# A macaron block on one core: Down's unpacking placed earlier in the first job, rows turned a step later, and a rearranged end

## The chip, the cores and the metric

The kernel runs on one core of one Trainium2 chip. A core has a matrix engine (TensorE, PE in the profile), a vector engine (VectorE, DVE), an activation engine (ScalarE, ACT), a general engine (GpSimd, POOL), and SyncE (SP), which here only issues transfers. They run side by side, each through its own instructions in order, and wait for each other by semaphores. Matrix products are written to PSUM, eight banks of 128 x 512 float32; everything else lies in SBUF, and transfers by DMA go between SBUF and DRAM. The metric is the device time of the whole kernel in microseconds, the median of several runs. Less is better.

## The reference

The input is 2 x 1024 tokens of 1024 features. Three sublayers follow each other: half a feed-forward, a state-space convolution, half a feed-forward.

```python
x = L0_attn_u
x = x + 0.5 * ffn(layernorm(x))
x = x + s4(layernorm(x))
x = x + 0.5 * ffn(layernorm(x))

def ffn(x):
    Wg, Wu, Wd = (dequant(...) for gate, up, down)   # 4-bit weights, a scale and a zero per 128 rows
    h = silu(xf @ Wg) * (xf @ Wu)                    # 1024 -> 2752
    return h @ Wd                                    # 2752 -> 1024

# dequant: W[k, n] = s[k // 128, n] * (w4[k, n] - (z4[k // 128, n] + 1))
# s4: a kernel K of length 1024 from its parameters, a causal convolution of each row with K, plus D * u
```

Eight 4-bit weights are packed in one 32-bit word along the rows of a weight matrix.

## The kernel before, in words

The 2048 tokens are four batches of 512. A feed-forward of one batch is a job, and there are eight: `JOBS = [(0, 1), (1, 1), (0, 3), (1, 3), (2, 1), (3, 1), (2, 3), (3, 3)]`, batch and sublayer. They are numbered 0 to 7 here. The convolution of a batch is woven into the first stage of a later job.

A job has two stages. Up (`gate_up`) takes 64 steps: eight waves of hidden columns, in each the eight groups of 128 input rows. Its input is the normalized batch, turned so that features lie on partitions, in two pieces of different precision (`xTh`, `xTl`), and each weight tile is multiplied with both. After each group the partial sums in PSUM (`pg`) are rescaled in place by a ratio of two groups' scales, some by ScalarE, some by VectorE (`scaled`, L811 and L815). So TensorE can only add the next group to a bank when that bank's rescale is done. At the end of a wave ScalarE and VectorE form `hf`, and GpSimd splits it in two pieces, `hh` and `hl`. Down (`down`) takes 44 steps, two halves of the output columns by 22 tiles of hidden rows. A step has four column groups `c` with two products each, into four banks `po`, with a rescale after each except for the last two of a half: tile 20 has none behind it, and after tile 21 (one product, the short tile) the result is scaled into `y`.

The weights of a step are signed bytes read from DRAM four steps ahead (`load_bytes`, L772 for Up, L779 for Down) and cast to float three steps ahead by GpSimd (`make_weights`, L788; in job 0 some by ScalarE, L786). The bytes are made once, during job 0: the packed words are fetched, their nibbles unpacked by VectorE with six operations (`signed_bytes`: two of L625, two of L629 that add the zero points, two of L632), copied by GpSimd (L670 for Up's eight blocks, L704 for Down's), and stored to DRAM (L676, L712). Down's words come in six blocks, three for each half of the output columns, named `rawd` in the profile, and in this text the first to the sixth. The third and the sixth have 88 rows instead of 128.

Instructions that belong to other work are hung on steps: `up` and `dn` are tables of hooks, run when the step's instructions are written; a number with a half is a hook in the middle of a step. `first_weights` hangs the unpacking. Its table `blocks` has a row per block: when its words are fetched, when the six VectorE operations come, when the eight copies; each second copy is followed half a step later by a store. The numbers count from Up step 52, and from 12 on they are Down steps less 12. What is written inside `in_order_of_writing`, `in_pieces` or `pinned` keeps its order on the named engine; everything else is ordered by a scheduler that works with estimated costs. So the order in which the engines finally run differs from the text, and where this text says that one instruction stands before another, it is the order of the built program. Fetches are moved forward by it as soon as their buffer is free. SyncE issues nearly all transfers of the kernel in one order, and a store that waits for its data holds up the loads behind it.

Job 0's Down stage also prepares job 1. The rows of batch 1 get their moments (L189, L192), `r` from `ve` by GpSimd (L205), a correction of `r` in four small VectorE operations, the first of them `e` (L218), the normalization by VectorE (`normalize`, L265), and they are turned by `turn_by_pool`: four transposes on TensorE (L239), a copy by ScalarE (L257), two operations of GpSimd (L258, L259). In jobs 1, 2, 5 and 6 the same correction for the batch of the job before is hung on the last steps of Up.

Results go back to the rows in two ways. In most stages `y` is turned by VectorE and DRAM. In the first half of job 0 and the second half of job 7 it is done by `back_by_products`: four transposes on TensorE (L1014) into a bank, and a sum on VectorE (L1016) onto the row tile `x`. The kernel ends with four of these, one for each tile of 128 rows, each followed by a store of its half row.

Of the kernel before, what the change touches and what calls it, by code (L numbers as in the profile page):

```python
# [57 lines left out]
def macaron_s4_kernel(  # L58
# [67 lines left out]
    def give_back(*tiles):  # L126
        for tile_ in tiles:
            i = held.pop(id(tile_))
            turn_of.remove(i)
            turn_of.append(i)  # L130
# [585 lines left out]
    def first_weights(up, dn, at):  # L716

        for w in range(1, len(WAVES)):  # L720
            s0 = (0, 4, 8 * w - (14 if w < 5 else 15))[min(w, 3) - 1]
            steps = (0.5, 1, 2.5, 3, 3) if w == 1 else range(6)
            in_pieces(at, [(up, s0 + d) for d in steps], lambda w=w: split(w))
            copies = {1: (3, 3, 3.5, 3.5) + (3.5,) * 4, 2: (3, 3, 4, 4, 5.5, 5.5, 6, 6)}
            copies = copies.get(w, (3, 3, 4, 5, 6, 6, 7, 8))
            if 1 < w < len(WAVES) - 1:
                both = lambda w=w: (fetch(w + 1), fetch_zeros(w + 1))
                at(up, s0 + (3 if w == 2 else 6), lambda both=both: in_order_of_writing(both, ET.SP))
            for k, d in zip(EVEN_FIRST, copies):
                at(up, s0 + d, lambda w=w, k=k: dequantize(w, k))  # L730
            for odd, o in enumerate({1: (3.5, 3.5), 2: (5.5, 7)}.get(w, (6.5, 9.5))):
                at(up, s0 + o, lambda w=w, odd=odd: keep_bytes(w, odd))
        s0 = len(STEPS) - 12

        def when(d):
            return (up, s0 + d) if d < 12 else (dn, d - 12)

        blocks = (
            (-3, (-1, -0.5, 0, 0.5, 1, 1.5), (1, 1, 2, 3, 4, 5, 6, 7)),
            (1, (3.5, 4, 5, 5.5, 6.5, 7.5), (8, 9, 10, 11, 12, 12, 13, 14)),  # L740
            (9, (13.5, 15, 16.5, 17.5, 19, 19.5), (18, 18, 18.5, 19, 20, 20, 21, 21.5)),
            (15, (20.5, 22, 23.5, 24, 25, 25.5), (24.5, 24.5, 25, 25.5, 26, 26.5, 27, 27.5)),
            (22, (27, 28.5, 30, 31, 31.5, 32.5), (31.5, 31.5, 32, 32.5, 33, 33.5, 34, 34.5)),
            (29, (35, 37, 39, 39.5, 41, 41.5), (40, 40.5, 41, 41.5, 42, 42.5, 43, 43.5)),
        )
        for k, (fetched, split_at, copied) in enumerate(blocks):
            a, rt = divmod(k, 3)
            at(*when(fetched), lambda a=a, rt=rt: fetch_down(a, rt))
            in_pieces(at, [when(d) for d in split_at], lambda a=a, rt=rt: split_down(a, rt))
            for i, (j, d) in enumerate(zip(EVEN_FIRST, copied)):  # L750
                at(*when(d), lambda a=a, rt=rt, j=j: dequantize_down(a, rt, j))
                if i % 2:
                    half = lambda a=a, rt=rt, i=i: keep_bytes_down(a, rt, i // 4, i // 2 % 2)
                    at(*when(d + 0.5), half)
# [180 lines left out]
    def down(j, b, hooks):  # L935

        steps = [(a, f) for a in range(NH) for f in range(NF)]
        for d, (a, f) in enumerate(steps):
            w = next_weights()
            for hook in hooks.get(d, ()):  # L940
                hook()
            if f == 0:
                ps = [acc(f"po_{j}_{a}_{c}") for c in range(4)]
            for c in range(4):
                if c == 2:
                    for hook in hooks.get(d + 0.5, ()):
                        hook()
                for k, part in enumerate(reversed(h[f])):
                    nc.tensor.matmul(  # L949
                        ps[c],  # L950
                        w[:, bass.ts(c, P)],
                        part,
                        start=(f == 0 and k == 0),
                        stop=(f == NF - 1),
                        skip_group_check=True,
                    )
                on_act = c % 2 == 0 or (j == 0 and c == 1 and f % 2 == 0)
                on_act = on_act or (c == 1 and d in relief.get(j, ()))
                if f < GD - 1:
                    scaled(on_act, ps[c], ps[c], ratd[:, 4 * a + c, f : f + 1])  # L960
                elif f == NF - 1:
                    if c == 0:
                        yT[a] = ypool.tile([P, 4 * TB], F32, tag="y", name=f"y_{j}_{a}")
                    if by_products(j, a):
                        y = yT[a][:, bass.ts(c, TB)]
                        scaled(on_act, y, ps[c], ratd[:, 4 * a + c, GD - 1 :])
                    else:
                        y, p = block_of(yT[a], c), ps[c].rearrange("p (t i) -> p t i", i=Q)
                        scaled(on_act, y, p, ratd[:, 4 * a + c, GD - 1 :])
                    give_back(ps[c])  # L970
        h.clear()

    by_products = lambda j, a: (j, a) in ((0, 0), (len(JOBS) - 1, NH - 1))
    y_dram = [dpool.tile([TB, 512], F32, tag=f"yz{a}", name=f"yz{a}") for a in range(NH)]
# [622 lines left out]
    def fast():  # L1597
        def store_half(t, a, queue):

            own = bass.ts(a, 512)  # L1600
            queue.dma_start(rows_of(out, JOBS[-1][0])[t][:, own], x[JOBS[-1][0]][t][:, own])

        for j, (b, k) in enumerate(JOBS):
# [4 lines left out]
            def at(hooks, s, f):  # L1608
                hooks.setdefault(s, []).append(f)

            if prev:
# [9 lines left out]
                if pk == 1:  # L1621
# [50 lines left out]
                    steps += [(up, start_ + gap * 3 + 14.5), (up, start_ + gap * 3 + 15)]  # L1672
                    in_pieces(at, steps, lambda: moments_by_tile(pb, 3, True, LIFT))
                    done = start_ + gap * 3 + 15
                    steps = [(up, done + 0.5 + i / (2 if j == 1 else 1)) for i in range(4)]
                    in_pieces(at, steps, lambda: deviations_in_pieces(pb, 3))

                    def save():
# [38 lines left out]
            if after:  # L1717
                ab, ak = after
                if ak == 1:
                    at(up, 55 if j == 0 else 6, lambda: load_x(ab, rows_of(u, ab)))  # L1720
                    if j == 0:
                        steps = [(dn, d) for d in (2.5, 4, 6, 9, 10.5, 14.5, 16, 17.5, 18.5)]
                        in_pieces(at, steps, lambda: moments_by_tile(ab, 1, True, LIFT))
                        steps = [(dn, 21 + i / 2) for i in range(4)]
                        in_pieces(at, steps, lambda: deviations_in_pieces(ab, 1))
                    else:
                        steps = [(up, s) for s in range(12, 21)] + [(up, 20.5)]
                        in_pieces(at, steps, lambda: moments_by_tile(ab, 1, True, LIFT))
                        steps = [(up, s) for s in range(21, 25)]
                        in_pieces(at, steps, lambda: deviations_in_pieces(ab, 1))  # L1730
                turns = {}

                def turning(t):
                    if t not in turns:
                        turns[t] = [], []
                        turns[t] += (turn_by_dma(ab, t, turns[t][1]),)
                    rest = turns[t][1] or turns[t][2:]
                    next(rest[0], None)

                for t in range(NT):  # L1740
                    for half in range(2):
                        d, where = (24 + 4 * t + 2 * half if j == 0 else (2, 6, 14, 20)[t] + half), dn
                        if j > 1:
                            d, where = (54 if ak == 3 else 25) + 2 * t + half, up
                        piece = lambda t=t, half=half: normalize(ab, t, half)
                        piece = lambda piece=piece: in_order_of_writing(piece, ET.DVE)
                        at(where, d, piece)
                    if j == 0:
                        for half in range(2):
                            piece = lambda t=t, half=half: turn_by_pool(ab, t, half)  # L1750
                            at(dn, 26 + 4 * t + 2 * half, piece)
                        continue
                    late = (12, 13) if t == NT - 1 else (13, 17)
                    for d in (1, 2, 3, 5, 6, 7, 9) + late:
                        piece = lambda t=t: turning(t)
                        piece = lambda piece=piece: in_order_of_writing(piece, ET.Pool, ET.SP)
                        at(dn, 2 + 9 * t + d + (j == 1 and t == 0), piece)
# [18 lines left out]
            down(j, b, dn)  # L1776
            assert all(s in (0, 0.5) or 0 <= s < len(STEPS) and s * 2 % 1 == 0 for s in up)
            assert all(0 <= d < NH * NF and d * 2 % 1 == 0 for d in dn)
        for t in range(NT):
            back_by_products(b, 1, t)  # L1780
            store_half(t, 1, (nc.sync, nc.scalar)[t % 2])

    STARTING = ET.Activation, ET.DVE, ET.SP
    first = {}
# [205 lines left out]
```

## Time and profile before

| What | Value |
|---|---|
| Runs, us | 2036.26, 2033.29, 2035.08; median 2035.08 |
| The profiled execution, us | 2036.95 |
| Its span, us | 2035.2 |
| Granted clock of TensorE, mean of the span | 0.998 |
| Job 0: Up's last products, Down's last products | about 185 us, 276.9 us |
| Busy of GpSimd, 240 to 250 us | 10.0 of 10 |
| Waits of PE for VectorE's rescales, whole span (Up, Down) | 4.7 us in 11, 3.1 us in 4 |
| Waits of GpSimd's casts for bytes of Down, whole span | 8.4 us in 5, 5.4 us in 3 of them in job 0 |
| TensorE's last product of Down | 2023.4 us |

The span runs from the first to the last instruction of the program; the time of an execution lies some 1.75 us above it. The time of runs differs by 3 us between the lowest and the highest. A line of the profile names the line of the kernel, the engine, the operation, and the tiles written and read (`po<-po,ratd`), with numbers of batch and step left out; a wait is put down to what ended it. PE's matmul times overlap, so that a product that is listed with 0.39 us follows the one before by 0.21 to 0.23 us.

### The profile page before, as it was taken

The page shows a single profiled execution, that of the slowest core. Times are in us where ns is not written, and L with a number is a line of the kernel's source. Part 1 is how long each engine was busy: PE and PEld are TensorE (multiplying, and loading weights), DVE is VectorE, ACT ScalarE, POOL GpSimd, SP SyncE. Part 2 cuts the span into 40 slices and gives each one's busy share as a digit, 9 for nine tenths or more (in the row PEclk, how much of TensorE's full clock was granted, in tenths as well). Part 3 has the DMA queues.
Part 4 walks back from the last instruction along what each step waited for, and adds up shares of the span by engine and source line. Part 5 has one row for each costly group of instructions (what it writes and reads, how often), then busy time and mean ns, then how long its engine had stood idle before and what let it go on. Part 6 is the DMA issues. An engine that isn't in the chain of part 4 may idle for free.

```text
span 2035.2 us, 29665 instructions
## 1 busy us (share of the span) xinstructions
PE 2004.1 (98%) x9202; PEld 1374.5 (68%) x9202; DVE 1631.0 (80%) x2710; ACT 1416.2 (70%) x2221; POOL 1371.5 (67%) x1771
## 2 busy tenths in 40 slices
PE   7999999999999999999999999999999999999998
PEld 4656766577766677656866578667686676866576
DVE  8987878868888778877778777887878878777776
ACT  7888787747775577777767776764776647767775
POOL 6977868748765577655976578754686646965542
PEclk9999999999999999999999999999999999999999
DMA  5343332343524236311552126242263331661113
GB/s 166 119 136 99 110 103 62 79 103 92 148 63 102 73 71 196 120 30 35 143 161 85 33 50 172 79 93 83 50 161 93 84 90 38 160 187 34 35 37 102
DMA packets 345965, 197.13 MB, mean 97 GB/s; under 512 B 166989, under 2 KB 323670, under 8 KB 345798
## 3 DMA queue, kind: packets, MB, share of 16 engines
q1 hardware_dynamic: 344206, 192.55, 34.9%
q10 hardware_dynamic: 1464, 2.20, 0.3%
q8 instruction: 75, 1.23, 0.3%
q14 instruction: 92, 0.75, 0.1%
q0 software_dynamic: 128, 0.39, 0.1%
HBM read 127.52 MB, written 48.57 MB: 87 GB/s over the span
## 4 chain that ended last, share of the span: by engine, by line
PE 93%; DVE 3%; POOL 1%; issue 1%; ACT 1%; DMA 0%; ACTq 0%; POOLq 0%; DVEq 0%
PE pg L855 58%; PE po L949 30%; PE pc L1317 3%; PE pb L1317 1%; ACT pg L811 1%; DVE pg L815 1%; DVE po L815 0%; POOL w_up L788 0%; DVE rawd L629 0%; POOL r L205 0%; DVE hf L890 0%; POOL hl L897 0%; DVE rawd L632 0%; DVE stats L1797 0%; POOL q L670 0%
## 5 line engine op out<-in xcount | busy, mean ns | idle before, releaser
L811 ACT ACTIVATE pg<-pg,rat 128x512 f32<-128x512 f32 x1280 | 807.1, 661 | 383.6 <-PE pg L855 378.8
L815 DVE TENSOR_TENSOR pg<-pg,rat 128x512 f32<-128x512 f32 x1128 | 748.2, 692 | 146.5 <-PE pg L855 139.1
L855 PE MATMUL pg<-xTh,w_up 128*128 128x512 f32 x2752 | 844.4, 435 | 3.9 <-DVE pg L815 2.7
L855 PE MATMUL pg<-xTl,w_up 128*128 128x512 f16 x2752 | 708.0, 381 | 2.5 <-DVE pg L815 2.0
L855 PEld LDWEIGHTS pg<-xTh,w_up 128*128 128x128 f32 x2752 | 518.4, 189 | 167.5 <-DVE pg L815 7.7
L788 POOL CAST w_up<-b 128x768 fp32r<-128x768 int8 (+2 forms) x491 | 376.6, 773 | 356.9 <-PE pg L855 259.1
L811 ACT ACTIVATE po<-po,ratd 128x512 f32<-128x512 f32 x669 | 438.2, 662 | 145.3 <-PE po L949 144.6
L949 PE MATMUL po<-hl,w_down 128*128 128x512 f32 x1344 | 527.5, 393 | 3.5 <-DVE po L815 3.1
L949 PE MATMUL po<-hh,w_down 128*128 128x512 f32 x1344 | 523.4, 390 | 0.0
L815 DVE TENSOR_TENSOR po<-po,ratd 128x512 f32<-128x512 f32 x611 | 424.4, 696 | 112.1 <-PE po L949 111.2
L855 PEld LDWEIGHTS <-w_up 128*128 128x128 bf16 x2752 | 226.7, 98 | 340.2 <-issue 156.1
L788 POOL CAST w_down<-bd 128x512 fp32r<-128x512 int8 x352 | 217.8, 623 | 151.6 <-PE po L949 73.7
L949 PEld LDWEIGHTS po<-hl,w_down 128*128 128x128 f32 x1344 | 252.5, 188 | 64.0 <-DVE po L815 8.3
L949 PEld LDWEIGHTS po<-hh,w_down 128*128 128x128 f32 x1344 | 252.8, 188 | 51.3
L897 POOL TENSOR_TENSOR hl<-hf,hh 128x512 fp32r<-128x512 f32 x168 | 217.1, 1292 | 7.1
L896 POOL CAST hh<-hf 128x512 fp32r<-128x512 f32 x168 | 108.3, 645 | 81.1 <-DVE hf L890 62.3
L890 DVE SCALAR_TENSOR_TENSOR hf<-pg,rat,g 128x512 f32<-128x512 f32 x168 | 121.1, 746 | 40.5 <-ACT g L887 34.3
L887 ACT ACTIVATE g<-pg,rat 128x512 f32<-128x512 f32 x168 | 110.1, 688 | 33.7 <-PE pg L855 17.8
L1002 POOL TENSOR_TENSOR x<-x,yr 128x512 f32<-128x512 f32 x52 | 66.8, 1284 | 0.0
L291 POOL TENSOR_TENSOR lo<-x,hi 128x512 f16<-128x512 f32 x48 | 62.0, 1291 | 0.0
L189 DVE BATCH_NORM_STATS2 stats<-x 128x6 f32<-128x512 f32 x88 | 60.0, 681 | 0.0
L289 POOL TENSOR_TENSOR mid<-hi,top 128x512 bf16<-128x512 f32 x48 | 56.0, 1167 | 0.0
(214 smaller groups left out, 1081.2 us busy)
## 6 DMA issues: line engine op xcount, KB each, us to landing
b<-wq SPq DMA_DIRECT2D x319, 96.0 KB
bd<-wdq SPq DMA_DIRECT2D x336, 64.0 KB
x<-in_L_attn_u_dram SPq DMA_DIRECT2D x30, 512.0 KB
yz<-y SPq DMA_DIRECT2D x56, 256.0 KB
yr<-yz SPq DMA_DIRECT2D x56, 256.0 KB
b<-wq SPq DMA_DIRECT2D x128, 64.0 KB
sz<-xn SPq DMA_DIRECT2D x16, 512.0 KB
st<-sz SPq DMA_DIRECT2D x64, 128.0 KB
```

Of the source, the lines that this page charges most:

```text
L291: nc.gpsimd.tensor_tensor(lo[:, own], n[:, own], hi[:, own].bitcast(F32), ALU.subtract)
L788: nc.gpsimd.tensor_copy(t, b)
L811: nc.scalar.activation(dst, src, AF.Copy, scale=sc)
L815: nc.vector.tensor_tensor(dst, src, sc.to_broadcast(list(dst.shape)), ALU.mult)
L855: product = lambda: nc.tensor.matmul(p, weights, (lo, hi)[k][:, g, :], start=(g == 0 and not done), stop=(g == GK - 1 and done), skip_grou ...
L887: nc.scalar.activation(g, pg, AF.Silu, scale=rat[:, 2 * f, GK - 1 :])
L890: nc.vector.scalar_tensor_tensor(hf, pu, last, g, ALU.mult, ALU.mult)
L896: nc.gpsimd.tensor_copy(hi, hf)
L897: nc.gpsimd.tensor_tensor(lo, hf, hi.bitcast(F32), ALU.subtract)
L949: nc.tensor.matmul(ps[c], w[:, bass.ts(c, P)], part, start=(f == 0 and k == 0), stop=(f == NF - 1), skip_group_check=True,)
L1002: nc.gpsimd.tensor_tensor(part, part, rows_back.pop((a, t)), ALU.add)
L1317: nc.tensor.matmul(dst, lhsT, rhs, start=start, stop=stop, skip_group_check=True)
```

## The change

Five places are edited.

- The table `blocks`: every number is lower, so the words of Down are fetched, unpacked, copied and stored sooner: two steps for the first block, three to three and a half for the third to fifth, four to five and a half for the sixth.
- In job 0 the normalization and the turning of batch 1's rows come one step later each.
- In jobs 2, 5 and 6 the first `e` operation comes one step later, at Up step 51.5, and the last of the four stays at 53.5. In job 1 the new formula gives the old steps.
- In the last job's second half, the last two tiles of hidden rows are handled together by a new function, `last_steps`: for each column group its three products, one behind the other, then the scaling into `y`. VectorE takes groups 0 and 2, ScalarE group 1, and group 3 is halved between them.
- At the very end the transposes of row tiles 0 and 3 are written first, without the last chunk, then their last chunk, then tiles 1 and 2. VectorE adds tiles 0, 1 and 2; tile 3 is copied from PSUM by ScalarE and added by GpSimd. The stores of tiles 0, 1 and 3 go to SyncE's queue, that of tile 2 to ScalarE's.

```diff
         blocks = (
-            (-3, (-1, -0.5, 0, 0.5, 1, 1.5), (1, 1, 2, 3, 4, 5, 6, 7)),
-            (1, (3.5, 4, 5, 5.5, 6.5, 7.5), (8, 9, 10, 11, 12, 12, 13, 14)),
-            (9, (13.5, 15, 16.5, 17.5, 19, 19.5), (18, 18, 18.5, 19, 20, 20, 21, 21.5)),
-            (15, (20.5, 22, 23.5, 24, 25, 25.5), (24.5, 24.5, 25, 25.5, 26, 26.5, 27, 27.5)),
-            (22, (27, 28.5, 30, 31, 31.5, 32.5), (31.5, 31.5, 32, 32.5, 33, 33.5, 34, 34.5)),
-            (29, (35, 37, 39, 39.5, 41, 41.5), (40, 40.5, 41, 41.5, 42, 42.5, 43, 43.5)),
+            (-5, (-3, -2.5, -2, -1.5, -1, -0.5), (-1, -1, 0, 1, 2, 3, 4, 5)),
+            (-1, (1, 2, 3, 4, 5, 6), (6, 7, 8, 9, 10, 10, 11, 12)),
+            (6, (10.5, 12, 13.5, 14.5, 16, 16.5), (15, 15, 15.5, 16, 17, 17, 18, 18.5)),
+            (12, (17.5, 19, 20.5, 21, 22, 22.5), (21.5, 21.5, 22, 22.5, 23, 23.5, 24, 24.5)),
+            (19, (24, 25.5, 27, 27.5, 28.5, 29.5), (28, 28, 28.5, 29, 29.5, 30, 30.5, 31)),
+            (25, (31, 32.5, 34, 34.5, 35.5, 36), (35, 35.5, 36, 36.5, 37, 37, 37.5, 38)),
         )
...
+            if (j, a) == (len(JOBS) - 1, NH - 1) and f >= GD - 1:
+                if f < NF - 1:
+                    before_last = w
+                else:
+                    last_steps(j, a, ps, before_last, w)
+                continue
...
+    def last_steps(j, a, ps, *ws):
+
+        y = yT[a] = ypool.tile([P, 4 * TB], F32, tag="y", name=f"y_{j}_{a}")
+        for c in range(4):
+            for f, w in zip((GD - 1, NF - 1), ws):
+                for part in reversed(h[f]):
+                    nc.tensor.matmul(
+                        ps[c],
+                        w[:, bass.ts(c, P)],
+                        part,
+                        start=False,
+                        stop=(f == NF - 1),
+                        skip_group_check=True,
+                    )
+            sc = ratd[:, 4 * a + c, GD - 1 :]
+            for i in range(2):
+                own = slice(TB * i // 2, TB * (i + 1) // 2) if c == 3 else slice(0, TB)
+                if c == 3 or i == 0:
+                    scaled((c + i) % 2, y[:, bass.ts(c, TB)][:, own], ps[c][:, own], sc)
+            give_back(ps[c])
...
-                    steps = [(up, done + 0.5 + i / (2 if j == 1 else 1)) for i in range(4)]
+                    steps = [(up, 62 + i / 2 if j == 1 else 51.5 + (3 * i // 2) / 2) for i in range(4)]
                     in_pieces(at, steps, lambda: deviations_in_pieces(pb, 3))
...
-                        d, where = (24 + 4 * t + 2 * half if j == 0 else (2, 6, 14, 20)[t] + half), dn
+                        d, where = (25 + 4 * t + 2 * half if j == 0 else (2, 6, 14, 20)[t] + half), dn
...
-                            at(dn, 26 + 4 * t + 2 * half, piece)
+                            at(dn, 27 + 4 * t + 2 * half, piece)
...
-        for t in range(NT):
-            back_by_products(b, 1, t)
-            store_half(t, 1, (nc.sync, nc.scalar)[t % 2])
+        turned_back = {}
+
+        def turn_back(t, *chunks):
+            if t not in turned_back:
+                turned_back[t] = bank(f"pb_{b}_1_{t}")
+            for c in chunks:
+                src = yT[1][:, bass.ts(c, TB)][:, bass.ts(t, P)]
+                nc.tensor.transpose(turned_back[t][:, bass.ts(c, P)], src, ident)
+
+        def last_products():
+            for t in (0, 3):
+                turn_back(t, 0, 1, 2)
+            for t in (0, 3):
+                turn_back(t, 3)
+            for t in (1, 2):
+                turn_back(t, 0, 1, 2, 3)
+
+        in_order_of_writing(last_products, ET.PE)
+        rows = gpool.tile([P, TB], F32, tag="g", name="last_rows")
+        nc.scalar.copy(by_block(rows), by_chunk(turned_back[3]))
+        part = x[b][3][:, 512:]
+        nc.gpsimd.tensor_tensor(part, part, rows, ALU.add)
+        for t in range(3):
+            part = by_block(x[b][t][:, 512:])
+            nc.vector.tensor_tensor(part, part, by_chunk(turned_back[t]), ALU.add)
+            pinned(lambda t=t: store_half(t, 1, (nc.sync, nc.sync, nc.scalar)[t]), ET.SP)()
+        pinned(lambda: store_half(3, 1, nc.sync), ET.SP)()
```

In the changed kernel the lines of `down` and below have other numbers; L625 to L855 keep theirs.

## The prediction

> **What bounds the kernel now.** First the page's busy times and its chain:
>
> ```profile
> PE 2004.1 (98%) x9202; PEld 1374.5 (68%) x9202; DVE 1631.0 (80%) x2710; ACT 1416.2 (70%) x2221; POOL 1371.5 (67%) x1771
> PE 93%; DVE 3%; POOL 1%; issue 1%; ACT 1%; DMA 0%; ACTq 0%; POOLq 0%; DVEq 0%
> ```
>
> TensorE is the bound; 31 us of the span have no matmul, 11 of them at the start and about 10 at the end. Only the few between, and the end, can be won. Second, the stages of job 0's Down (us, length, busy of each engine; the 0.93, 0.90, 1.00, 0.52 are the granted clock):
>
> ```profile
> 240.00:250.00 10.00, 7.26 (x30) 5.29 (x30) 8.78 (x8) 6.01 (x10) 10.00 (x15) 0.93 0.13 28
> 250.00:260.00 10.00, 10.00 (x49) 8.24 (x48) 6.52 (x10) 6.94 (x12) 8.21 (x12) 0.90 0.51 154
> 244.50:248.50 4.00, 1.53 (x7) 0.97 (x6) 3.95 (x3) 1.34 (x3) 4.00 (x7) 1.00 0.23 54
> 248.50:252.00 3.50, 3.50 (x12) 2.68 (x11) 1.60 (x3) 1.32 (x2) 3.50 (x6) 0.52 0.18 39
> ```
>
> PE loses 10 - 7.26 = 2.7 us, GpSimd is full, and right behind PE runs at half clock. Third, the chain in that stretch, the word-unpacking line's durations (minimum/median/maximum ns), and what GpSimd ran:
>
> ```profile
> 243.48 0.61 DVE po L815
> 244.09 3.05 DVE rawd L632
> 247.15 0.61 DVE po L815
> 247.76 0.04 issue
> 247.81 3.96 PE po L949 x10
> ```
> ```profile
> L632 DVE TENSOR_SCALAR rawd<-rawd x12: 410/418/3136, 161.1 to 244.0; 128x1024 uint16<-128x1024 uint16 x8, 88x1024 uint16<-88x1024 uint16 x4
> ```
> ```profile
> 243.91 0.61 POOL L704 COPY qd<-rawd 88x512 int8<-88x512 int8 x1
> 244.48 1.27 POOL L259 TENSOR_TENSOR xTl<-turn,xTh 128x512 f16<-128x512 f32 x1
> 245.71 0.61 POOL L704 COPY qd<-rawd 88x512 int8<-88x512 int8 x1
> 246.26 1.36 POOL L788 CAST w_down<-bd 128x512 fp32r<-128x512 int8 x2
> ```
>
> One unpacking operation of the sixth block took 3.14 us against a median of 0.42 while GpSimd went from instruction to instruction. The rescale behind it on VectorE came late, and PE stood. Fourth, a smaller stall that recurs at 698, 1426 and 1685 us (VectorE, then PE):
>
> ```profile
> 1684.64 0.55 DVE L218 TENSOR_TENSOR e<-r 128x4 f32<-128x4 f32 x1 [0.53 <-POOL r L205]
> 1685.12 1.28 DVE L815 TENSOR_TENSOR pg<-pg,rat 128x512 f32<-128x512 f32 x2
> ```
> ```profile
> 1685.86 0.50 PE L855 MATMUL pg<-xTh,w_up 128*128 128x512 f32 x1 [0.67 <-DVE pg L815]
> ```
>
> Last, the end (chain, then the store queue of ScalarE):
>
> ```profile
> 2023.95 1.36 PE pb L1014 x10
> 2025.31 0.02 issue
> 2025.34 1.36 DVE x L1016 x3
> 2026.69 0.44 issue
> 2027.13 0.68 DVE x L1016
> ```
> ```profile
> 2026.65 1.54 ACTq L1601 DMA_DIRECT2D out_dram<-x  x2
> ```
>
> Four sums of 0.62 us run one after another behind the transposes, and the last store starts at 2027.8.
>
> **The change, part by part.** The sum is made against the profiled execution, 2036.95 us (span 2035.2 and 1.75 around it), which is 1.9 above the median of the runs, 2035.08; I take it off the median. A Down step is 1.85 us (eight matmuls on the chain).
>
> A, the unpacking. Per block six VectorE operations, eight GpSimd copies of 0.61, four stores and the fetches move two to five steps. GpSimd's demand explains the jam: a cast (0.61) a step, from step 26 a turn every second step (0.61 + 1.28), and in steps 28 to 31 the sixth block's eight copies: per step 0.61 + 0.95 + 1.22 = 2.8 us in 1.85. Afterwards the copies stand in steps 23 to 26, 0.61 + 1.22 = 1.83, and turns begin at 27, 0.61 + 0.95 = 1.56. Both fit, and the block's two-byte operations (L629 and L632, steps 22 to 24) mostly precede its copies. So the 2.7 us go, and with them the half clock: 3.5 x (1 - 0.52) = 1.7. Together -4.4; bounds 0 (a like jam elsewhere) and -4.4.
>
> The trace has PE slow right after 2.7 us without work. [...]
>
> A', the rest of job 0. PE's idle time, by the same view, is 0.54 and 0.68 in 140 to 160 and 160 to 180, and 0.23 and 0.32 in 200 to 220 and 220 to 240, the marks of unpacking operations of 0.6 to 1.2 us ahead of a rescale. They move with the operations. Three operations of the second block (0.42 to 1.23 each) now fall before wave 6 ends, where VectorE idled only 1.6 us outside its wait for ScalarE, but they leave wave 7. I take 0; bounds -1.8 (all gone) and +1.8 (doubled). The fetches are no term: the first two blocks' words leave SyncE at 137 and 138 us and are first touched at 157.5, two steps sooner now; the sixth's leave at 200.3 and the new first use is step 19, about 220.
>
> B, the three late `e`. In jobs 2, 5 and 6 `e` moves one step back and stands behind two more rescales (1.28) where r was late by 0.53. The 0.67 us go three times: -2.0; bounds 0 (the wait only moves) and -2.5 (1.06 us from product to product there, against 0.21 elsewhere). The last piece ends half a step ahead of the normalization that needs it, as before.
>
> C, the end. In the last two steps each column group is finished before the next, so three of four are scaled early; the fourth is halved over ScalarE and VectorE (0.41 for 256 columns, L1008). The last chunk is there at about 2024.4 instead of 2024.7, and only two transposes stand between it and the first sum: about 2024.75 against 2025.34. Three sums end at 2026.6; beside them ScalarE's copy (0.59, L257's row) and GpSimd's sum (1.28, L1002) end at 2026.9. The last store starts 0.9 sooner. The stores share the DMA engines (1 MB from 2027.0 to 2030 us), which starts 0.6 sooner with the first store. I take -0.9, nearer to the last store; bounds -0.3 and -1.2.
>
> D, rows turned a step later. The last converted piece ended at 272.94; 1.85 and four transposes (0.44) later is 275.2, and job 1's first product starts at 276.90. ScalarE's copy (0.59) moves to steps with two rescales, where a third one had filled 2.4 us, VectorE's normalization (0.54 to 0.93) to steps with two: 2 x 0.61 + 0.93 = 2.15 in 1.85 + 0.44. Covered: 0. Bounds: -0.5, ScalarE's overflow of one such step, and +1.5, a late first product of job 1 or eight rescales late by 0.2.
>
> Sum: -4.4 + 0 - 2.0 - 0.9 + 0 = -7.3, so 2027.8 us (the profiled execution: 2029.7).
>
> **Rivals.** R1, the jam moves. Other VectorE operations stand beside a full GpSimd, the fifth block's at steps 15 to 17 and the normalizations; one held as at 244 gives back A. B and C alone are -2.9: 2032.2, within 0.2% (4 us, about what a measurement can tell from no change). For it: GpSimd stays at 84 to 99% in steps 23 to 41. Against: of twelve operations of L632 only one was over 0.9. [...] The trace has 3.14, past three ends of GpSimd instructions.
>
> R2, slower: loads queued behind stores on SyncE. The load for up step 62 now stands behind one store, 63's behind four, and Down's loads 13 to 15, 20, 27 to 29 and 34 to 37 between stores that each wait for two copies. Casting runs three steps ahead, 5.5 us; a load took 1.9 (issued 235.42, cast from 237.28) and a cast 0.6, which leaves 3.0. A store later than that stops PE, at up to 2.7 + 1.7 = 4.4; two and a half such stops decide, three give 2027.8 + 13.2 = 2041. Against: copies come 5 us earlier against the step that loads them, and the waits for stored bytes (5.4 us, three times in job 0) show that this distance was the short one.
>
> R3, the half clock stays for another reason: A is -2.7, the time 2029.5.
>
> **How the numbers follow.** The forecast has 0.69, R3 0.07, R1 0.14, R2 0.10: faster 0.76, same 0.14, slower 0.10. Low end: -4.4 - 1.8 - 2.5 - 1.2 = -9.9, and 0.4 of the runs' spread: 2024.8. High end: R1 with half of D: 2033.0. R2 and the corners, under 0.2, are left out.
>
> **What would show it.** In the profile after: no L632 over 1.3 us and PE busy over 9.7 in each 10 us of 220 to 270, at clock 1.00 (A); no 0.67 us before a product near 698, 1426 and 1685 (B); the last store 3.1 us behind the end of PE's last Down product instead of 4.0 (C); job 1's first product without a wait (D). A new stall of PE over 2 us in job 0 makes it wrong; if VectorE ends it, it is R1, if a cast or a load does, R2.

## The result and the profile after

| | before | after |
|---|---|---|
| Median of 14 runs each, us | 2036.18 (2032.37 to 2037.51) | 2031.47 (2030.43 to 2033.41) |
| Ratio, 95% interval | | 0.9977 (0.9970 to 0.9984) |
| Profiled execution, us (its span) | 2036.95 (2035.2) | 2031.49 (2029.6) |

The change is 4.7 us faster by the medians and 5.5 between the profiled executions, inside the range and on the side that was forecast; -7.3 had been forecast. The forecast of 2027.8 was counted from a median of three runs, 2035.08; over 14 runs it is 1.1 higher. The page's first part and chain:

```profile
PE 2002.4 (99%) x9202; PEld 1372.3 (68%) x9202; DVE 1628.9 (80%) x2710; ACT 1415.6 (70%) x2222; POOL 1371.5 (68%) x1772
PE 95%; DVE 3%; ACT 1%; POOL 0%; issue 0%; DMA 0%; ACTq 0%; DVEq 0%
```

TensorE stays the bound, with 95% of the chain instead of 93%. The stages of job 0's Down (start and end, length, busy of PE, PEld, DVE, ACT, POOL, then clock, DMA share, GB/s), first after, then the first stretch of before, which the prediction did not show:

```profile
190.00:200.00 10.00, 9.52 (x41) 7.08 (x40) 9.78 (x17) 7.73 (x13) 9.66 (x14) 1.00 0.24 67
220.00:230.00 10.00, 9.99 (x43) 7.37 (x42) 8.97 (x18) 6.63 (x12) 8.79 (x13) 1.00 0.59 168
230.00:240.00 10.00, 8.90 (x39) 6.41 (x38) 8.35 (x14) 7.23 (x12) 7.83 (x13) 1.00 0.32 87
240.00:250.00 10.00, 10.00 (x50) 8.19 (x49) 6.58 (x11) 8.70 (x15) 7.40 (x11) 1.00 0.28 84
250.00:260.00 10.00, 10.00 (x54) 8.39 (x53) 6.97 (x11) 7.99 (x14) 7.38 (x10) 1.00 0.31 105
```
```profile
190.00:200.00 10.00, 10.00 (x45) 8.21 (x44) 8.79 (x16) 8.72 (x14) 7.25 (x12) 1.00 0.15 41
```

The jam at 245 and the half clock behind it are gone: 10.00 instead of 7.26, clock 1.00. But PE now loses 0.5 in 190 to 200 and 1.1 in 230 to 240, where it had lost 0.0 and 0.2. The unpacking line and PE's waits for rescales of Down after:

```profile
L632 DVE TENSOR_SCALAR rawd<-rawd x12: 409/648/1480, 159.5 to 234.8; 128x1024 uint16<-128x1024 uint16 x8, 88x1024 uint16<-88x1024 uint16 x4
```
```profile
PE po L955 <- DVE po L815: 1.8, 4, 0.7
```

The longest operation fell from 3.14 to 1.48 us, while the median rose from 0.42 to 0.65. There is one long hold less, and more short ones. (An operation is called held where it takes clearly longer than the same operation does elsewhere.) VectorE, GpSimd and PE at two of the places:

```profile
191.44 1.48 DVE L632 TENSOR_SCALAR rawd<-rawd 88x1024 uint16<-88x1024 uint16 x1
192.84 0.68 DVE L189 BATCH_NORM_STATS2 stats<-x 128x6 f32<-128x512 f32 x1
193.44 1.27 DVE L815 TENSOR_TENSOR po<-po,ratd 128x512 f32<-128x512 f32 x2
...
232.58 1.70 DVE L629 TENSOR_TENSOR rawd<-rawd,zd 88x1024 uint16<-88x1024 uint16 x1
234.21 0.68 DVE L815 TENSOR_TENSOR po<-po,ratd 128x512 f32<-128x512 f32 x1
```
```profile
191.35 1.28 POOL L897 TENSOR_TENSOR hl<-hf,hh 128x512 fp32r<-128x512 f32 x1
...
231.46 2.27 POOL L704 COPY qd<-rawd 88x512 int8<-88x512 int8 x4 [0.34 <-DVE r L224]
233.69 1.06 POOL L788 CAST w_down<-bd 128x512 fp32r<-128x512 int8 x1
```
```profile
194.17 0.50 PE L955 MATMUL po<-hl,w_down 128*128 128x512 f32 x1 [0.48 <-DVE po L815]
...
234.95 0.50 PE L955 MATMUL po<-hl,w_down 128*128 128x512 f32 x1 [0.72 <-DVE po L815]
```

At 191.44 an operation that elsewhere takes 0.41 runs beside a GpSimd sum of 1.28 that began 0.09 us sooner; the rescale behind it is late and PE waits 0.48. At 232.58 it is the same beside four copies, 1.70 where it is 0.68 at its shortest, and PE waits 0.72. The end, as the chain has it:

```profile
2016.63 2.74 PE po L985 x12
2019.38 0.02 issue
2019.40 0.48 ACT y L811
2019.88 0.02 issue
2019.91 0.44 DVE y L815
2020.34 0.04 issue
2020.39 0.78 PE pb L1813 x5
2021.17 0.02 issue
2021.19 0.68 DVE x L1830
2021.87 0.82 POOL x L1827
```

The two halves of the fourth column group, meant to run side by side, run one after the other (0.48, then 0.44).

Where the 5.5 us between the two spans lie, from the starts of the stages in the traces: job 0's Up +0.84, its Down -2.72, jobs 2, 5 and 6 -0.85, -0.88 and -0.86, the other jobs +0.02 together, and -1.09 behind the last product.

### The profile page after: what moved, and what is told of

It reads as the page before. It is cut to its first block, busy times and chain, and to the rows that moved or that the text cites. A ratio compares the mean times of both kernels' runs of the same rounds, so it can differ in the third digit from the quotient of the medians.

```text
span 2029.6 us, 29690 instructions
## 1 busy us (share of the span) xinstructions
PE 2002.4 (99%) x9202; PEld 1372.3 (68%) x9202; DVE 1628.9 (80%) x2710; ACT 1415.6 (70%) x2222; POOL 1371.5 (68%) x1772
## 3 DMA queue, kind: packets, MB, share of 16 engines
q10 hardware_dynamic: 1320, 1.94, 0.3%
## 4 chain that ended last, share of the span: by engine, by line
PE 95%; DVE 3%; ACT 1%; POOL 0%; issue 0%; DMA 0%; ACTq 0%; DVEq 0%
PE pg L855 60%; PE po L955 30%; PE pc L1344 3%; PE pb L1344 1%; DVE pg L815 1%; ACT pg L811 0%; DVE po L815 0%; DVE rawd L629 0%; DVE stats L1848 0%; PE pt L239 0%; POOL q L670 0%; DMA raw<-in_L_ffn_up_qweight_dram 0%; DVE rawd L632 0%; DVE r L224 0%; PE po L985 0%
## 5 line engine op out<-in xcount | busy, mean ns | idle before, releaser
L855 PE MATMUL pg<-xTh,w_up 128*128 128x512 f32 x2752 | 844.4, 435 | 1.9 <-DVE pg L815 0.7
L855 PE MATMUL pg<-xTl,w_up 128*128 128x512 f16 x2752 | 707.6, 381 | 2.4 <-DVE pg L815 2.0
L855 PEld LDWEIGHTS pg<-xTh,w_up 128*128 128x128 f32 x2752 | 518.4, 189 | 166.1 <-ACT pg L811 7.2
L855 PEld LDWEIGHTS <-w_up 128*128 128x128 bf16 x2752 | 226.9, 98 | 339.6 <-issue 154.4
```

The source lines that it names most:

```text
L855: product = lambda: nc.tensor.matmul(p, weights, (lo, hi)[k][:, g, :], start=(g == 0 and not done), stop=(g == GK - 1 and done), skip_grou ...
```

## The experiments

All compute the same as the kernel before. "Down of job 0" is the time from its first product to job 1's first, in the profiled execution. The runs of before beside them had medians of 2035.92 (e1 to e4), 2036.62 (e5 to e8) and 2036.87 (e9 to e12).

| Run | Edit | Median, us | Ratio to before, 95% | Down of job 0, us |
|---|---|---|---|---|
| before | | 2036.18 | 1 | 91.56 |
| after | all | 2031.47 | 0.9977 (0.9970, 0.9984) | 88.85 |
| e1 | unpacking and turning alone | 2034.06 | 0.9992 (0.9983, 1.0001) | 89.83 |
| e2 | corrections alone | 2035.09 | 0.9995 (0.9986, 1.0004) | 91.83 |
| e3 | end alone | 2036.04 | 1.0004 (0.9996, 1.0013) | 87.22 |
| e4 | unpacking alone | 2034.32 | 0.9992 (0.9983, 1.0001) | 89.61 |
| e5 | before, fifth block a step sooner | 2034.66 | 0.9996 (0.9986, 1.0005) | 91.61 |
| e6 | before, four copies on ScalarE | 2032.76 | 0.9986 (0.9977, 0.9994) | 87.48 |
| e7 | after, fourth group whole | 2031.90 | 0.9979 (0.9970, 0.9988) | 89.91 |
| e8 | e5, corrections, end of e7 | 2034.02 | 0.9990 (0.9981, 0.9999) | 86.85 |
| e9 | after, old corrections | 2034.93 | 0.9992 (0.9983, 1.0001) | 89.78 |
| e10 | after, only the sixth row sooner | 2032.33 | 0.9984 (0.9975, 0.9993) | 89.98 |
| e11 | before, two operations half a step sooner | 2033.60 | 0.9990 (0.9981, 0.9999) | 87.49 |
| e12 | e6, corrections, end of e7 | 2030.83 | 0.9977 (0.9967, 0.9986) | 87.06 |

The interval of the ratio takes in 1 for e1 to e5 and e9, so their medians alone do not tell them from before; what they show rests on the profiles and on how the runs group.

The theory at the start: job 0's gain was given back in part (A' was mis-sized), and the jam at 245 is a matter of chance. The rival: A came whole and the loss lies elsewhere.

**The parts alone.** e1 has the two edits of job 0, e4 only the table `blocks`, e2 the line of the corrections, e3 `last_steps` and the rows of the end.

> Only job 0 is changed: the earlier unpacking and the later turning; the corrections and the end are those of before. The stage times of the two profiles put -1.9 us on job 0: -4.3 of the stall and the half clock at 245 to 252, given back in part by smaller stalls at 158, 193, 231 and 234 (about +1.8) and by 0.6 that lies ahead of the first moved instruction. Theory 1, A' was mis-sized: -1.2 to -2.5 us against before by the medians. Theory 2, the stall at 245 is a matter of chance (four of the 14 runs of before lie 3 to 4 us under the others): the median gains more or less as those runs fall, but the runs of this kernel lie within 2 us of each other, without a lower group. Rival: A came as forecast, -4.4, and the loss against the forecast lies elsewhere.

> Only the table of the unpacking is changed; rows are turned at the old steps. If D costs nothing, the time is that of the run with both, -1.2 to -2.5 us against before, and no operation of unpacking is over 1.5 us. Rival: the later turning is what keeps GpSimd below its limit: turns begin at step 26 beside the sixth block's last copies, a stall of 1 to 3 us stands between 236 and 245 us, and the gain is 0 to -1.

> Only the first e operation of jobs 2, 5 and 6 is one step later. Theory 1: the profile's -0.85, -0.88 and -0.86 in these three jobs is all theirs: -2.6 us, a little over the bound of -2.5 on record. Rival: half of it comes from elsewhere in these jobs: -1.3. By theory 2 job 0 keeps its two groups of runs, 3 to 4 us apart, as in the kernel before.

> Only the end is changed, the finished column groups and the rows. Theory 1: -1.15 us, the difference of the two profiles from TensorE's last product of Down to the end of the span (11.8 to 10.6); in its profile the fourth group's two halves run one behind the other (0.47 + 0.42) as in the changed kernel. Rival: the stores share the same transfer time, and only 0.3 to 0.7 is left. By theory 2 job 0 keeps its two groups of runs.

e1 is 1.9 us under before, as by the first theory, and its runs (2032.79 to 2035.38) form one group. e4 is 0.3 above e1, within their spread, with the same stalls (PE lost 1.1 in 230 to 240 in both) and none of 1 to 3 us between 236 and 245: turning a step later neither costs nor saves anything that can be seen.

e2 and e3 gave less than expected, -0.8 and +0.1 by the medians. Their medians are of two things. The runs of before, 116 in all, fall in two groups: 29 lie under 2034.1 us with a mean of 2032.9, the others over 2034.7 with a mean of 2036.7. e2 had one run of 12 clearly below the rest, 2029.71, e3 two of 11. The profile of e3 shows what the lower group is. All of job 0 is the program of before there, in the same order on every engine, and yet (stage, then VectorE, then GpSimd):

```profile
240.00:250.00 10.00, 10.00 (x51) 8.07 (x50) 8.90 (x13) 8.57 (x16) 10.00 (x15) 1.00 0.13 28
```
```profile
243.12 0.79 DVE L632 TENSOR_SCALAR rawd<-rawd 88x1024 uint16<-88x1024 uint16 x1
```
```profile
243.02 0.61 POOL L258 CAST xTh<-turn 128x512 fp32r<-128x512 f32 x1
243.58 0.80 POOL L704 COPY qd<-rawd 88x512 int8<-88x512 int8 x1
244.35 1.29 POOL L259 TENSOR_TENSOR xTl<-turn,xTh 128x512 f16<-128x512 f32 x1
```

GpSimd is as full as in the profile before (10.00), and PE loses nothing. The same operation ended 0.28 us behind the end of the cast (243.63), and the copy behind was held instead (0.80 against 0.61). Job 0's Down is 4.34 us shorter, which is what A had been priced at. The courses have parted one operation sooner, at L629 (before, then e3):

```profile
241.78 1.70 DVE L629 TENSOR_TENSOR rawd<-rawd,zd 88x1024 uint16<-88x1024 uint16 x1
```
```profile
241.92 0.68 DVE L629 TENSOR_TENSOR rawd<-rawd,zd 88x1024 uint16<-88x1024 uint16 x1
```

So the jam is one of two courses of the same program, in about three of four executions, if each run of the lower group is like the one of e3 that was profiled.

**What decides the course?** In the profiles with the jam (before, e2) the loads behind the fifth block's last store left SyncE 3.8 and 3.7 us after that store, in e3 2.0. The queue of SyncE, before and e3:

```profile
235.42 3.18 SPq L779 DMA_DIRECT2D bd<-wdq  x7
```
```profile
233.71 4.00 SPq L779 DMA_DIRECT2D bd<-wdq  x7
```

The store itself left at 231.65 and 231.73. This made a theory: a late store shifts GpSimd's casts by half a us, and with that the phase, which here means where in GpSimd's instructions a VectorE operation begins. Two edits tested it, together with a whole fourth group and a combination:

```diff
 e5
-            (22, (27, 28.5, 30, 31, 31.5, 32.5), (31.5, 31.5, 32, 32.5, 33, 33.5, 34, 34.5)),
+            (21, (26, 27.5, 29, 30, 30.5, 31.5), (30.5, 30.5, 31, 31.5, 32, 32.5, 33, 33.5)),
 e6
-        nc.gpsimd.tensor_copy(by_chunk(...), by_block(src))
+        copy = nc.scalar.copy if (a, rt) == (1, 2) and j % 4 >= 2 else nc.gpsimd.tensor_copy
+        copy(by_chunk(...), by_block(src))
 e7
-            for i in range(2):
-                own = slice(TB * i // 2, TB * (i + 1) // 2) if c == 3 else slice(0, TB)
-                if c == 3 or i == 0:
-                    scaled((c + i) % 2, y[:, bass.ts(c, TB)][:, own], ps[c][:, own], sc)
+            scaled(c % 2, y[:, bass.ts(c, TB)], ps[c], sc)
```

> Only the fifth block (fetch, unpacking, copies, stores) is one step sooner; the sixth block, whose unpacking jams at 245, stays where it was before. Theory 1, the late store: in the profiles with the jam the fifth block's last store released the loads of tiles 30 and on 3.7 us after its issue, in the one without it 2.0 us, with the same order of instructions; the cast of tile 30 then came 0.5 us late and GpSimd's work met the unpacking in another phase. With 1.9 us more room that cast no longer waits for bytes: the lower group alone is left, 2032 to 2034, median 2032.9, no stall of PE over 1 us in 236 to 255 and no half clock. Rival: GpSimd's demand at the sixth block is enough by itself; two groups stay and the median is within 1 us of before.

> Before, with four of the sixth block's eight copies on ScalarE instead of GpSimd; the late store stays as it was. Theory A (full GpSimd): the jam needs both the late store and a GpSimd without gaps; with 4 x 0.6 us less on it between 240 and 252 us no unpacking operation is over 1.7 us and the runs form one group at 2032 to 2034, ScalarE's copies (4 x 0.6) costing at most 1 us. Rival, the phase alone: one GpSimd instruction after another at the wrong moment is enough, two groups stay, 3 to 4 us apart.

> The changed kernel with the fourth column group of the end scaled whole by ScalarE (0.69) instead of in two halves, which ran one behind the other (0.47 + 0.44). Theory: from TensorE's last product of Down to the issue of the last store 0.2 us less, 3.1 instead of 3.3, and the median 0.2 lower, 2031.3. Rival: the halves were serial for a reason that also holds a whole one (VectorE's scaling of the third group), no difference.

> The table of before with the fifth block one step sooner, rows turned at the old steps, the later corrections and the new end with a whole fourth group. Theory 1: the lower group of before (2032.9), less 2.3 of the corrections, 0.7 of the end and 0.2 of the whole group: 2029.7, below the changed kernel (2031.5). Rival (demand alone): the jam comes in most runs, 2033 to 2033.5 by the median.

The late store fell. In e5 the loads left at 233.01, 2.0 us behind the store, and the jam came all the same, in the profile and in six of 12 runs (2035.55 to 2038.52; the others 2031.56 to 2033.78). VectorE and GpSimd of e5:

```profile
243.96 3.14 DVE L632 TENSOR_SCALAR rawd<-rawd 88x1024 uint16<-88x1024 uint16 x1
```
```profile
237.22 0.61 POOL L788 CAST w_down<-bd 128x512 fp32r<-128x512 int8 x1 [3.59 <-DMA bd<-wdq]
```

A cast still waited for a load and began at 237.22, as before at 237.28. e8, whose only difference in job 0 is that of e5, has both groups too, 2029.26 to 2030.76 in four runs and 2034.02 to 2035.82 in six (one at 2032.27). Its profile is of the run of 2029.26 and has no jam: GpSimd busy for 10.00 of 240 to 250, and L632 0.79 at 243.12. In job 0 every engine runs the same instructions in the same order as in e5, whose profile, of a run of 2036.67, has the jam. e6 has one group, 11 runs from 2032.54 to 2034.61, and no L632 operation over 0.90 us in its profile: with four copies less on GpSimd the jam does not come.

e7: from the start of the last product to the issue of the last store it is 3.60 us, after 3.75, all kernels with the old end 4.43. The halves did cost 0.15. That is too little for the medians.

**Demand or phase.** e6 fits both a GpSimd that is too full and one whose instructions fall otherwise. e11 leaves GpSimd its work and moves two VectorE operations; e10 moves only the sixth block; e9 and e12 price the corrections and the sum of parts.

```diff
 e11
-            (29, (35, 37, 39, 39.5, 41, 41.5), (40, 40.5, 41, 41.5, 42, 42.5, 43, 43.5)),
+            (29, (35, 37, 39, 39.5, 40.5, 41), (40, 40.5, 41, 41.5, 42, 42.5, 43, 43.5)),
 e9 (from after)
-                    steps = [(up, 62 + i / 2 if j == 1 else 51.5 + (3 * i // 2) / 2) for i in range(4)]
+                    steps = [(up, done + 0.5 + i / (2 if j == 1 else 1)) for i in range(4)]
```

e10 is after with the first five rows of `blocks` as before, and e12 joins the lines of e6, e7, the new corrections and the new end to before.

> Before, with the last two operations of the sixth block half a step sooner; GpSimd has the same work. Theory B (phase): whether the operation is held depends on what GpSimd begins just ahead of it, so the share of runs in the upper group (about 7 in 10 before) becomes another, near 0 or near 1, with the groups still 3 to 4 us apart. Theory A (full GpSimd): its demand is the same, the share stays about 7 in 10 and the median within 1 us of before.

> The changed kernel with the first five rows of the unpacking table as before; only the sixth block is sooner. Theory: the losses at 193 and 199 us (0.64 and 0.71) come from the third block's operations among the late tiles of the first half and go; those at 232 and 234 (0.54 and 0.88) come from the sixth block beside the turning and stay or grow, since the fifth block's last operations now lie beside it; no jam at 245. Median 0.5 to 1.3 under the changed kernel, 0.9972 of before. Rival: sixth and fifth together fill GpSimd, and a stall of 2 to 4 us comes between 230 and 242: 0 to 2 us above the changed kernel.

> The changed kernel with the corrections of jobs 2, 5 and 6 at their old steps: no jam at 245 blurs the medians, so the difference to the changed kernel (0.9977 of before) is the price of B alone, and the difference to the run of job 0's part alone (0.9992) that of C alone. Theory: the three profiles with the new corrections have 0.80 to 0.92 us less in each of the three jobs, so this kernel is 2.4 us above the changed one, 0.9989 of before, and C is worth 0.6. Rival: the corrections' gain is not seen in the whole, as in the run of the corrections alone (0.9995 of before): 1 us, 0.9982.

> The table of before, with four of the sixth block's copies on ScalarE, the later corrections and the new end with a whole fourth group. If the parts add: 2032.8 for the copies alone, less 2.4, 0.6 and 0.2: 2029.6, one group of runs, 0.997 of before and 1.5 to 2 us under the changed kernel. Rival: the phase is chance, and the copies' single group does not hold with other corrections and another end: two groups, median 2032 to 2034.

e11 decides for the phase. In the built program the two operations stand one rescale sooner, and GpSimd's order is that of before up to 246 us. All 11 runs lie from 2033.07 to 2034.36, and GpSimd is as full as ever (columns as above, then VectorE and GpSimd):

```profile
240.00:250.00 10.00, 9.71 (x48) 7.52 (x47) 9.16 (x14) 7.91 (x14) 10.00 (x16) 1.00 0.16 37
```
```profile
243.21 0.79 DVE L632 TENSOR_SCALAR rawd<-rawd 88x1024 uint16<-88x1024 uint16 x1
```
```profile
243.11 0.61 POOL L258 CAST xTh<-turn 128x512 fp32r<-128x512 f32 x1
243.67 0.80 POOL L704 COPY qd<-rawd 88x512 int8<-88x512 int8 x1
```

A full GpSimd is thus not enough for a jam. Two numbers of the table, moved by half a step, took it away as the whole rewritten table did, and without the small stalls: job 0's Down is 87.49 against 88.85 to 89.91.

e10 was expected to lose the stalls at 193 and 199 and to keep those at 232 and 234. The first went, PE loses 0.1 in 190 to 200; but a single stall of 2.7 us came in place of the others, 16 us ahead of the old one, with a half clock behind it (PE, stage, VectorE):

```profile
232.37 0.51 PE L955 MATMUL po<-hl,w_down 128*128 128x512 f32 x1 [2.71 <-DVE po L815]
```
```profile
230.00:240.00 10.00, 7.63 (x26) 6.08 (x27) 8.02 (x13) 4.83 (x9) 10.00 (x16) 0.83 0.63 181
```
```profile
229.28 1.12 DVE L629 TENSOR_TENSOR rawd<-rawd,zd 88x1024 uint16<-88x1024 uint16 x1
230.33 0.56 DVE L222 SCALAR_TENSOR_TENSOR f<-e 128x4 f32<-128x4 f32 x1
230.81 0.41 DVE L632 TENSOR_SCALAR rawd<-rawd 88x1024 uint16<-88x1024 uint16 x1
231.15 0.56 DVE L224 SCALAR_TENSOR_TENSOR r<-f,r 128x4 f32<-128x4 f32 x1
231.63 1.28 DVE L815 TENSOR_TENSOR po<-po,ratd 128x512 f32<-128x512 f32 x2
```

No operation is held for 3 us here: two of the unpacking and two of the correction of `r` stand in a row, 2.35 us ahead of the rescale. Three of them are held a little: L629 takes 1.12 us where 0.64 is its shortest, L222 and L224 take 0.56 where their medians are 0.15. So it is a queue of short holds, not one long one. The stall is as long as that of the jam, but job 0's Down is 89.98, 1.6 less than with the jam. It was the rival of that expectation by place and size. The runs did not show the expected gain of 0.5 to 1.3 over the changed kernel: e10 is 4.5 us under its before, after 4.7.

e9 is 2034.93, 1.94 under its before, after is 4.71 under its own: B is worth 2.8 by medians, 2.6 by the stages of the profiles. e1 to e9 is C by medians: 0.1, in a spread that hides it. e12 is 6.0 us under its before by the median, e7 and after 4.7; its ratio, 0.9977, has the same middle as that of after and an interval of plus or minus 0.1%. It does not measurably beat the changed kernel, and the expected 1.5 to 2 us under it did not come. Eight runs lie at 2029.95 to 2031.18 and two at 2032.6 and 2032.7, which is less apart than the groups of before; the two were not profiled, so what they are stays open.

## Why the prediction was right or wrong

The forecast's -7.3 and the profiles' -5.5: A -4.3 for -4.4, A' +2.5 for 0, B -2.6 for -2.0, C -1.1 for -0.9, D 0. That the miss is only 1.8 is in part luck: B and C came out larger and took 0.8 off the 2.5 that A' had wrong.

**A** had the right size, but in three of four executions only, and its cause was taken too simply. "GpSimd's demand explains the jam" fails: e3, e8 and e11 have the same demand and no jam. What is shown is that a full GpSimd is not enough (10.00 of 10 us in e3 and e11, with L632 at 0.79), that the phase decides (e5 and e8 have the same order on every engine and differ in time alone, L632 taking 3.14 us in one and 0.79 in the other), and that a shift of half a step, four copies less on GpSimd, or the new table each end it; whether a GpSimd with gaps could jam is not separated, since e6 changed both demand and phase. Since the median of before lies in its upper group, the medians hide the part of chance almost wholly: against the mean of the lower group, 2032.9, the changed kernel's 2031.5 is only 1.4 faster.

**A' is the step that failed**: "They move with the operations... I take 0", bounded by a doubling (+1.8). Of the profiles without the new table and its early sixth row, the five without the jam (e3, e6, e8, e11, e12) have 86.85 to 87.49 us for job 0's Down, those of the new table 88.85 to 89.91. Against the 87.22 of e3 the new table costs 1.6 in the changed kernel's own profile, which is inside the bound, and 2.4 to 2.7 in the four others, which is outside it. The rest of the +2.5, 0.84 in Up, is mostly chance: 0.6 of it lies before 130 us, ahead of any moved operation, and behind that point the five profiles with the new table lose 0.20 to 0.23 in Up, each against the profile before. The error was to price the moved operations by their own time. The stretch of 190 to 200 us, where the third block's last operations now stand, had VectorE at 8.79 and GpSimd at 7.25 of 10 us; after it is 9.78 and 9.66. There an operation of 0.41 takes 1.48, at 232.58 one of 0.68 takes 1.70, and a rescale stands behind each. Rival R1, "the jam moves", was this in small: not one hold of 3 us but four stalls of 0.5 to 0.9 (0.64, 0.71, 0.54 and 0.88 at 193, 199, 232 and 234, counted from product to product), 2.8 where all come, against its 4.4; the profile of after lacks that at 199. Two marks set for A failed: PE was to be over 9.7 in every 10 us from 220 to 270 and had 8.90 in 230 to 240, and no L632 was to be over 1.3 us, where the longest took 1.48.

**B** was right in mechanism and too small: the term was the wait of 0.67, but a product that waited cost 0.85 from start to start against its neighbours, three times; the prediction had that figure as its bound (-2.5). The six profiles with the later corrections have 2.1 to 2.6 less in these three stages. After, `e` finds its `r`:

```profile
1680.44 1.40 DVE L815 TENSOR_TENSOR pg<-pg,rat 128x512 f32<-128x512 f32 x2 [0.18 <-PE pg L855]
1681.75 0.15 DVE L218 TENSOR_TENSOR e<-r 128x4 f32<-128x4 f32 x1
1681.96 0.70 DVE L815 TENSOR_TENSOR pg<-pg,rat 128x512 f32<-128x512 f32 x1
```

**C** had been -0.9 by the last store, which now leaves 0.68 sooner behind the last product: 3.35 us behind its end, where 3.1 had been the mark and 4.04 was before. The step that was wrong is "the fourth is halved": the halves do not overlap, and e7 with the whole group is 0.15 better. In the built program VectorE's half waits for ScalarE's: in the trace VectorE stood 0.50 us until that one was done, and the two took 0.48 and then 0.44. The prediction had not counted this wait. Both halves read one bank; whether that is the reason, or something else that they share, no run shows. The time from the last store's issue to the end of the span, 6.4 to 8.0 us over the fourteen profiles without order, blurs the rest.

**D** was right: job 1's first product starts at 275.02 without a wait, and e4 against e1 shows no price.

**R2** did not come. No load or cast stops PE; GpSimd's waits for bytes in job 0 fell from 5.4 us in three to 1.6 in one. **R3** is refuted: the half clock went with the stall (1.00 in 240 to 260 us after, where it had been 0.93 and 0.90), and came back with another in e10 (0.83 in 230 to 240).

## What to carry to other kernels

Where two engines hold each other, as L632 (3.14 us for 0.41) and GpSimd's copy (0.80 for 0.61) were held here, take several executions before pricing a stall: this one was in about three of four, and half a step decided it. An operation that moves beside a busy engine that can hold it is priced by its held time there, not by its own: 1.48 us for 0.41 here with VectorE at 9.78 and GpSimd at 9.66 of 10 us, and 1.70 for 0.68 beside four copies; the smallest edit that breaks the phase should be tried ahead of a shift of everything, as e11 against e1 shows for this one case. Count what stands ahead of a rescale on its engine, since in e10 four short operations made as long a stall (2.71 us) as one that was held for 3 us (2.47).

## What was unexpected of the hardware

In the traces of before and after, each change of the clock lies a whole multiple of 3.413 us, to within 0.1 of one, behind its first rise. In before the clock rose at 16.53 us (L1841's products of 0.42 us became 0.27); the half clock came 68 such lengths later, at 248.64, lasted one, 3.413 us, and came again at the end after 590. In after it rose at 13.94 (L1892, 0.42 to 0.27) and fell only at the end, after 589. The clocks in the rows of e2 (0.98 and 0.85 in the two stretches from 240 to 260), e5 (0.87 and 0.96 there) and e10 (0.83 from 230 to 240) make 3.4 us at half clock each. In before PE had waited 2.47 us for a rescale and gone on at 247.81, 0.83 us ahead of the half clock; its longest wait in the stretch was 2.4 in e2, 2.5 in e5 and 2.71 in e10, while the stalls of 0.54 to 0.88 in after left the clock at 1.00. In e5, by an estimate from its row (0.87 is 2.6 us at half clock up to 250), it began at about 247.4, some 0.3 us before the rescale that PE waited for was done (247.71).

The hold of 3.14 us was the same in three profiles (before, e2, e5), to within 0.01, past the ends of three GpSimd instructions; in before it ended 0.28 us behind the end of a fourth (246.87). In e3 and e11 the operation ended 0.28 us behind the first such end and took 0.79. In all five it had begun 0.10 us behind the start of a GpSimd instruction, a copy in the jam and the cast L258 without it. That it was a copy does not decide: in e8 it also began 0.10 us behind the start of a copy, and took 0.79. What lets VectorE in at one boundary and not at another was not tried and stays open, as does what sets the phase from run to run.
